# A two-layer graph network on one core: sums carried between spans inside PSUM, one register load per span, transfers addressed in bytes

## The chip, the cores and the metric

The kernel runs on one core of one Trainium2 chip. The metric is the device time of one execution in microseconds. A core has five engines that run side by side, each through its own queue of instructions in order: PE multiplies matrices, DVE and ACT work on rows of data, POOL here issues nothing but gathers (indirect transfers), and SP issues the plain transfers. Engines wait for each other through semaphores. The transfers themselves are moved by 16 DMA engines.

## The reference, cut to what matters

```
h = relu(layernorm(x))
# layer 0
edge_in  = concat(h[src], h[dst], edge_attr)
m        = relu(relu(edge_in @ We1 + be1) @ We2 + be2)
node_msg = relu(relu(concat(h[dst], m) @ Wn1 + bn1) @ Wn2 + bn2)
x1 = x + h + segment_sum(node_msg, dst)
# layer 1
h = relu(layernorm(x1))
H = einsum('ni,rio->rno', h, W)
out = x1 + relu(segment_sum((H[etype, src] + b[etype]) * weight, dst))
```

There are N = 12,500 nodes of 128 floats and E = 400,000 edges, sorted by dst, with 64 edge attributes and 8 edge types. Everything is float32.

## The kernel before

**Tiling.** Edges are taken in chunks of 1024 (8 tiles of 128 edges); three chunks are a span. There are 391 chunks and 131 spans. As edges are sorted by dst, the edges of one span end in at most 128 consecutive nodes, beginning at the span's least dst. So a span sums its messages into a 128-row window `acc` in PSUM with matmuls against one-hot matrices (L467 in layer 0, L937 in layer 1). Neighbouring spans share a node where their edges meet: a window of the next span begins on a row that the span before has already added to. The window's place is known only at run time: the least dst of each chunk (`cidx`, already times 3) and of each span (`span`) lie in SBUF, and SP loads them into registers.

**Preamble (0 to about 130 us).** It builds tables of projected nodes (`tab_a`, `tab_cb`), the ends of the chunks, `cidx`, `span`, and a flag `bad` for inputs on which the fast path does not hold. A slower path (`again`) follows under that flag and is not entered with these inputs.

**Layer 0 (about 130 to 5430 us, L698–L728 and its end to L775).** One iteration i of the loop works on chunks i to i-3 at once. POOL gathers chunk i (L357, 8 gathers of 128 rows into `gb`, buffers for 16 chunks; DVE's L402 transposes them and frees them). PE and ACT run the edge network through `pre` (L395, L397), `h` (L410), `pm` (L417), `em` (L422), `u` (L428, L431), `h` (L434), `pq` (L441); DVE adds and multiplies (L449, L455), builds the one-hot matrices (L381, L460), and PE sums the chunk into `acc` (L467). At the end of a span:

- DVE adds the window's old sums `aw`, loaded from `agg0_d` (L474), and the two halves of `acc` into `a20` (L479, L480); SP stores `a20` back to `agg0_d` (L656). This is how a shared row reaches the next span. For that `agg0_d` is filled with zeros first, by 25 transfers of 256 KB (L690–L693).
- `rows_h` (L508–L530) makes x1 = x0 + a20 (L511) and stores it to `x1_d` (L512), normalises it, multiplies by the 8 weight matrices (L520, L528, L529), and stores 128 rows of 8 x 128 floats to `tab_h` (L530).

SP's queue in one span of layer 0, in its order: tab_h (L530), agg0_d (L656), x1_d (L512), then for the coming chunks eats (edge attributes of a span, 768 KB, L555, 3 buffers), relb (756 KB, L557), win (L377, three), xt (L643) and aw (L474): 10 transfers. Each row number is a register load (L549 for each chunk, L639 for the span), and each transfer with a row number has address arithmetic in registers before it. That makes 37 instructions in one row, which all stand behind tab_h's wait for DVE's ht (L529).

**Layer 1 (about 5430 to 9827 us, `layer1_once`, L903–L988).** POOL gathers 8 tiles of `tab_h` rows (512 bytes each) per chunk (L963, buffers for 5 chunks), DVE weighs and adds them (L970, L974), and PE sums the two end segments into `acc` (L937). Per span SP loads the row number (L952), xw from `x1_d` (L956) and aw from `agg_d` (L944), stores agg_d (L806) and out (L809). DVE adds aw and both halves of acc (L804, twice) and makes out (L808).

**Order.** `in_order` (L92–L101) fixes the order of SP, DVE, ACT and PE as the program is written, layer by layer; POOL's order is its program order as well. All buffers are released by semaphores.

Of the kernel before, what the change touches and what calls it, by code (L numbers as in the profile page):

```python
# [11 lines left out]
I32 = mybir.dt.int32  # L12
AF = mybir.ActivationFunctionType
# [9 lines left out]
R = 8  # L23
N = 12500
# [22 lines left out]
NONE = 16384  # L47

@with_exitstack
def gnn_kernel(  # L50
# [33 lines left out]

    nc = tc.nc
# [25 lines left out]
    x1_d = dram.tile([NP + P, D], F32, name="x1_d")  # L111
    agg_d = dram.tile([NP + P, D], F32, name="agg_d")
    tab_h = dram.tile([NP + P, R * D], F32, name="tab_h")
# [29 lines left out]
    cidx = const.tile([1, NCP], I32, name="cidx")  # L143
# [4 lines left out]
    base = const.tile([P, NSP], F32, name="base")  # L148

# [6 lines left out]
    while g < NJ:  # L156
        n = min(GJ if g else 4, NJ - g)
        groups.append((g, n))
        g += n

# [98 lines left out]
    with tc.tile_pool(name="n1", bufs=2) as pool:  # L259
# [56 lines left out]
        nc.vector.tensor_scalar(cidx, los, 3.0, None, op0=OP.mult)  # L316
        nc.vector.tensor_reduce(slo, los.rearrange("o (s c) -> o s c", c=SC), AX.X, OP.min)
        nc.vector.tensor_reduce(shi, his.rearrange("o (s c) -> o s c", c=SC), AX.X, OP.max)
        nc.vector.tensor_copy(span, slo)
# [12 lines left out]
        vs = pool.tile([1, 5], F32, name="vs", bufs=1)  # L332
# [10 lines left out]
        nc.vector.tensor_reduce(vs[:, 2:3], v3, AX.X, OP.max)  # L343
        nc.vector.tensor_copy(vs[:, 3:4], slo[:, 0:1])
        nc.vector.tensor_scalar(vs[:, 4:5], slo[:, NS - 1:NS], -1.0, float(N - P),
                                op0=OP.mult, op1=OP.add)
        nc.vector.tensor_reduce(vm[:, 0:1], vs, AX.X, OP.max)

# [13 lines left out]
    class Edges:  # L362
# [7 lines left out]
        def load(self, c, row):  # L370
            self.eat = self.pool.tile([P, 512], F32, name="eat", bufs=2)
            nc.sync.dma_start(self.eat, ea[ds(c, 1), :, :].rearrange("o k e -> (o k) e"))
            self.load_win(row)

        def load_win(self, row):
            self.win = self.pool.tile([WR, 96], BF16, name="win", bufs=8)
            nc.sync.dma_start(self.win, tab_cb[ds(row, WR), :])  # L377

        def ends_T(self):
            self.ohT = self.pool.tile([WR, CE], BF16, name="ohT", bufs=4)  # L380
            nc.vector.tensor_tensor(self.ohT, self.relb, self.node.to_broadcast([WR, CE]),  # L381
                                    op=OP.is_equal)
# [10 lines left out]
        def first(self):  # L393
            self.pre = self.psum.tile([64, 512], F32, name="pre")
            nc.tensor.matmul(self.pre, w_ea, self.eat, start=True, stop=False)  # L395
            for h in range(2):
                nc.tensor.matmul(self.pre[32 * h:32 * h + 32, :], self.win[:, 64:96],  # L397
                                 self.half_T(h), start=False, stop=True)
# [64 lines left out]
        def fifth(self, acc, start, stop):  # L463
            for i in range(CT):

# [3 lines left out]
                                 start=(start and i == 0), stop=(stop and i == CT - 1))  # L469

# [37 lines left out]
    def rows_h(pool, psum, row, x0, aw, banks, to_out=False):  # L508

        x1 = pool.tile([P, D], F32, name="x1", bufs=2)  # L510
        nc.vector.tensor_add(x1, x0, aw)  # L511
        nc.sync.dma_start(x1_d[ds(row, P), :], x1)  # L512
        if to_out:
            nc.sync.dma_start(out[ds(row, P), :], x1)
# [8 lines left out]
        ht = pool.tile([P, R * D], F32, name="ht1", bufs=2)  # L523
# [6 lines left out]
        nc.sync.dma_start(tab_h[ds(row, P), :], ht)  # L530


    with tc.tile_pool(name="e0", bufs=2) as pool, \
# [6 lines left out]
        chunks, spans, loaded = {}, {}, {}  # L540
        active = []

# [3 lines left out]

        def load(c):
            e = Edges(pool, psum, iota_p, nid_p)
            row = nc.values_load(cidx[0:1, c:c + 1], engines=[ENG.SP], min_val=0,  # L549
                                 max_val=3 * (N - 1),  # L550
                                 skip_runtime_bounds_check_because="a chunk's least dst is a node")
            s, k = divmod(c, SC)
            if k == 0:
                eat = pool.tile([P, SC, 512], F32, name="eats", bufs=3)
                nc.sync.dma_start(eat, ea[c:c + SC, :, :].rearrange("c k e -> k c e"))  # L555
                relb = pool.tile([WR, SC, CE], BF16, name="relb", bufs=2)
                nc.sync.dma_start(relb, rel_d[c:c + SC, :].rearrange("(o c) e -> o c e", o=1)  # L557
                                  .to_broadcast([WR, SC, CE]))
                loaded[s] = eat, relb
            eat, relb = loaded[s]  # L560
            e.eat, e.relb = eat[:, k, :], relb[:, k, :]
            e.load_win(nc.s_assert_within(
                row, 0, 3 * (NP - WB), skip_runtime_bounds_check_because="WB < NP - N"))
            chunks[c] = e

        def prepare():
# [5 lines left out]
            for g in range(0, NTP, QT):  # L572
                m = min(QT, NTP - g)
                cols = slice(g, g + m)
                for given, table in ((dst_t, dst_d), (et, hidx_d), (ew, ew_d)):
# [6 lines left out]
                    elif given is et:  # L582
                        nc.vector.scalar_tensor_tensor(raw[:, :m], src_sb[:, cols], float(R),
# [48 lines left out]
            nc.sync.dma_start(x1_d[NP:NP + P, :], zeros[:, 0, :])  # L632
            yield from zero(zeros, agg_d)

        class Span:


            def __init__(self, s):
                self.row = nc.values_load(  # L639
                    span[0:1, s:s + 1], engines=[ENG.SP], min_val=0, max_val=N - 1,  # L640
                    skip_runtime_bounds_check_because="a span's least dst is a node")
                self.xt = pool.tile([P, D], F32, name="xt")
                nc.sync.dma_start(self.xt, x[ds(self.row, P), :])  # L643
# [4 lines left out]
            def begin(self):  # L648
                self.x0 = plus_normed(pool, self.xt, self.mv, self.sd)
                self.aw = window0(pool, self.row, P)  # L650

            def end(self, left):

                a2 = add0(pool, self.aw, self.acc, P)
                if left:
                    nc.sync.dma_start(agg0_d[ds(self.row, P), :], a2)  # L656
                banks = ("u", "u", "u") if left else ("pre", "pm0", "pm1")
                steps = rows_h(pool, psum, self.row, self.x0, a2, banks)
# [7 lines left out]
        def sum_up(c):  # L666
# [5 lines left out]
            chunks.pop(c).fifth(of.acc, k == 0, stop)  # L672
# [15 lines left out]
        for c in range(min(AHEAD, NC)):  # L688
            load(c)
        zeros = pool.tile([P, 4, D], F32, name="zeros", bufs=1)  # L690
        nc.vector.memset(zeros, 0.0)
        for _ in zero(zeros, agg0_d):
            pass  # L693
        chunks[0].ends_T()
# [3 lines left out]
        for i in range(L):  # L698
            if i + AHEAD < NC:
                load(i + AHEAD)  # L700
            if i % SC == 0 and i:
                spans[i // SC - 1] = Span(i // SC - 1)
            gb = gathered(i)
            chunks[i].first()
# [9 lines left out]
            chunks[i + 1].ends_T()  # L714
# [23 lines left out]
        for s in range((L - 1) // SC, NS):  # L738
            if s not in spans:
                spans[s] = Span(s)  # L740
                spans[s].deviate()
        spans[(L - 1) // SC].begin()
        gb = gathered(L)
        chunks[L].first()
# [34 lines left out]
    tab_hr = tab_h[0:N, :].rearrange("n (r o) -> (n r) o", r=R)  # L779
# [13 lines left out]
    def window1(pool, row):  # L793

        aw = pool.tile([P, D], F32, name="aw")
        nc.sync.dma_start(aw, agg_d[ds(row, P), :])
        xw = pool.tile([P, D], F32, name="xw1")
        nc.sync.dma_start(xw, x1_d[ds(row, P), :])
        return aw, xw

    def add_out(pool, aw, xw, accs, row):
        a2 = pool.tile([P, D], F32, name="a2")
        for acc in accs:
            nc.vector.tensor_add(a2, aw, acc)  # L804
            aw = a2
        nc.sync.dma_start(agg_d[ds(row, P), :], a2)  # L806
        o = pool.tile([P, D], F32, name="o")
        nc.vector.scalar_tensor_tensor(o, a2, 0.0, xw, op0=OP.max, op1=OP.add)  # L808
        nc.sync.dma_start(out[ds(row, P), :], o)  # L809
# [22 lines left out]
    def again():  # L832
# [7 lines left out]
        with tc.tile_pool(name="g1", bufs=2) as pool, \  # L840
                tc.tile_pool(name="g1_ps", bufs=1, space=PSUM) as psum:

            def layer0(s):
# [5 lines left out]
                def body(row):  # L849
                    acc = psum.tile([P, 2 * D], F32, name="acc")  # L850
                    for k in range(SC):
                        c = s * SC + k
                        e = Edges(pool, psum, iota_f, nid)
                        e.load(c, row * 3)
                        e.ends_T_of(c, node)
                        e.first()
# [18 lines left out]
            with tc.For_i(0, NP, P) as row:  # L875
# [3 lines left out]
                for _ in rows_h(pool, psum, row, x0, window0(pool, row, P), ("u", "u", "u"),  # L879
                                to_out=True):  # L880
                    pass

        with tc.tile_pool(name="g2", bufs=2) as pool, \
                tc.tile_pool(name="g2_acc", bufs=2, space=PSUM) as accp:

            def layer1(s):
# [4 lines left out]
                def body(row):  # L891
# [4 lines left out]
                    add_out(pool, *window1(pool, row), (acc,), row)  # L896
# [6 lines left out]
    def layer1_once():  # L903


        WS = 4
        with tc.tile_pool(name="e1", bufs=2) as pool, \
# [6 lines left out]
            sums_of = []  # L914
# [16 lines left out]
            def sum_up(acc, sm, hm, rel, begin, stop):  # L931
# [4 lines left out]
                for q in range(2):  # L936
                    nc.tensor.matmul(acc[:, 0:2 * D], oh[:, q, :],  # L937
# [3 lines left out]
            def write():  # L941
                acc, row, xw = sums_of.pop(0)
                aw = pool.tile([P, D], F32, name="aw")
                nc.sync.dma_start(aw, agg_d[ds(row, P), :])  # L944
                return lambda: add_out(pool, aw, xw, (acc[:, 0:D], acc[:, D:2 * D]), row)

            for c in range(NC):
                s, k = divmod(c, SC)
                if k == 0:
                    if s % WS == 0:  # L950
                        w_p = weights(s)
                    row = nc.values_load(  # L952
                        span[0:1, s:s + 1], engines=[ENG.SP], min_val=0, max_val=N - 1,
                        skip_runtime_bounds_check_because="a span's least dst is a node")
                    xw = pool.tile([P, D], F32, name="xw1", bufs=3)
                    nc.sync.dma_start(xw, x1_d[ds(row, P), :])  # L956
                    acc = psum.tile([P, 512], F32, name="acc1", bufs=3)
                    sums_of.append((acc, row, xw))
                    if s:
                        end = write()  # L960
# [18 lines left out]
                todo.append((acc, sm, hm, ends, k == 0, k == SC - 1 or c == NC - 1))  # L979
                if k == SC - 1 and s:  # L980
                    end()
# [76 lines left out]
```

## Time and profile before

| what | us or share |
|---|---|
| median of 3 runs (lowest, highest) | 9830.73 (9818.11, 9840.15) |
| the profiled execution's own time | 9828.86 |
| its span | 9827.1 |
| PE busy; DVE; ACT; POOL | 38%; 54%; 17%; 64% |
| granted PE clock, mean | 0.657 |
| gathers of layer 0 (L357), 3032 of them | 2865.2, 945 ns each |
| gathers of layer 1 (L963), 3128 of them | 3327.2, 1064 ns each |

And the page's busy shares along the span, in 40 slices of 246 us, where a digit is tenths:

```profile
PE   2566666666666666666667100000000000000000
PEld 1223333323333332332333000000000000000000
DVE  4556655555555555555557555555555555555554
ACT  2222222222222222222223000000000000000000
POOL 6555555555555555555552677777777777777776
PEclk6777777777777778777778555555555555555555
DMA  4333333222222222222222222222222222222221
```

The first 22 slices are layer 0, the others layer 1. In layer 0 PE, DVE and POOL are each busy for half to two thirds; in layer 1 POOL leads and PE is nearly idle. A busy share is a mean over a slice: what an engine waits for has to be read from the waits and the timeline. A wait "<-remote" is one whose semaphore event the profile cannot lay to an instruction of this core.

### The profile page before, as it was taken

To read this page: it belongs to the slowest core of one execution; us is meant where nothing else is said; L and a number is where in the kernel's file an instruction comes from. 1 tells how busy PE (TensorE), PEld (TensorE's weight loads), DVE (VectorE), ACT (ScalarE), POOL (GpSimd) and SP (SyncE) were. 2 spreads that over 40 slices of the span, in tenths; PEclk is the share of its full clock that TensorE was granted. 3 is DMA by queue.
4 is the path that set the end of the run, shared out by engine and by line. 5 is a ranking of instruction groups with operands and counts; after the bars stand their busy time and mean duration, and the time that the engine had idled before them with its cause. 6 is when DMAs were issued, how large, how long until landed. Compare 5 with 4: busy or idle time off the path is not lost.

```text
span 9827.1 us, 59273 instructions
## 1 busy us (share of the span) xinstructions
PE 3767.4 (38%) x13461; PEld 1854.1 (19%) x13462; DVE 5327.9 (54%) x8545; ACT 1659.8 (17%) x3217; POOL 6320.1 (64%) x6273
## 2 busy tenths in 40 slices
PE   2566666666666666666667100000000000000000
PEld 1223333323333332332333000000000000000000
DVE  4556655555555555555557555555555555555554
ACT  2222222222222222222223000000000000000000
POOL 6555555555555555555552677777777777777776
PEclk6777777777777778777778555555555555555555
DMA  4333333222222222222222222222222222222221
GB/s 150 75 83 78 76 78 94 75 69 70 69 70 73 75 70 69 70 70 70 69 73 83 59 55 55 55 55 55 55 55 55 55 55 55 55 55 55 55 55 50
DMA packets 706959, 662.00 MB, mean 67 GB/s; under 512 B 372896, under 2 KB 561124, under 8 KB 706142
## 3 DMA queue, kind: packets, MB, share of 16 engines
q1 hardware_dynamic: 504440, 401.06, 13.1%
q0 software_dynamic: 200192, 256.65, 12.3%
q8 instruction: 110, 1.80, 0.1%
q14 instruction: 253, 2.07, 0.1%
q10 hardware_dynamic: 1964, 0.41, 0.0%
HBM read 527.08 MB, written 130.51 MB: 67 GB/s over the span
## 4 chain that ended last, share of the span: by engine, by line
POOL 31%; PE 21%; another core or an unknown queue 18%; issue 18%; DVE 7%; ACT 5%; DMA 1%; SPq 0%; DVEq 0%; ACTq 0%; POOLq 0%
POOL hg L963 31%; PE pq L441 5%; PE pm L417 3%; PE acc L467 3%; PE pre L395 3%; PE u L431 2%; DVE nm L455 2%; ACT em L422 2%; PE u L528 2%; ACT h L434 1%; PE pre L397 1%; ACT h L410 1%; DVE ht L529 1%; PE u L428 1%
## 5 line engine op out<-in xcount | busy, mean ns | idle before, releaser
L357 POOL DMA_INDIRECT gb<-tab_a,src_sb x3032 | 2865.2, 945 | 2220.2 <-DVE agT L402 1359.8
L963 POOL DMA_INDIRECT hg<-tab_h,hidx_sb x3128 | 3327.2, 1064 | 1198.4 <-issue 1001.8
L970 DVE TENSOR_TENSOR v<-hg,io_p 128x1024 f32<-128x1024 f32 x782 | 960.1, 1228 | 2135.4 <-DMA hg<-tab_h,hidx_sb 2127.5
L937 PE MATMUL acc<-hm,oh 128*128 128x256 f32 x782 | 299.8, 484 | 4067.7 <-DVE oh L934 2162.8
L449 DVE TENSOR_TENSOR pq<-pq,b_n 128x512 f32<-128x512 f32 x782 | 529.7, 696 | 1430.2 <-remote 991.7
L937 PEld LDWEIGHTS acc<-hm,oh 128*128 128x128 f32 x782 | 196.0, 311 | 4172.4 <-issue 4138.0
L974 DVE TENSOR_REDUCE sm<-v 128x128 f32<-128x1024 f32 x782 | 959.1, 1227 | 9.0
L441 PE MATMUL pq<-w_n,h 128*128 128x256 f32 x3128 | 871.3, 429 | 0.0
L977 ACT CAST hm<-sm 128x256 fp32r<-128x256 f32 x391 | 145.5, 372 | 4224.2 <-DVE sm L974 3662.8
L455 DVE SCALAR_TENSOR_TENSOR nm<-pq,nm 128x512 fp32r<-128x512 f32 x782 | 503.9, 686 | 600.4 <-ACT nm L450 424.4
L434 ACT ACTIVATE h<-u,b_n 128x512 f32<-128x512 f32 x391 | 268.6, 687 | 2649.9 <-remote 1726.3
L441 PEld LDWEIGHTS pq<-w_n,h 128*128 128x128 f32 x3128 | 663.2, 223 | 95.9 <-issue 0.8
L417 PE MATMUL pm<-h,w_e 32*128 32x512 f32 x1564 | 550.6, 786 | 106.6 <-ACT h L410 71.5
L422 ACT ACTIVATE em<-pm,b_e 128x512 f32<-128x512 f32 x782 | 492.8, 680 | 530.0 <-PE pm L417 399.9
L467 PE MATMUL acc<-nm,oh 128*128 128x256 f32 x3128 | 572.4, 335 | 23.7 <-DVE ht L529 4.9
L395 PE MATMUL pre<-eats,w_ea 128*64 128x512 f32 x782 | 537.5, 776 | 85.8 <-DMA eats<-in_ea 84.8
L467 PEld LDWEIGHTS acc<-nm,oh 128*128 128x128 f32 x3128 | 483.4, 229 | 411.0 <-issue 157.6
L520 PE MATMUL u<-ident,t 128*128 128x128 f32 x130 | 56.8, 437 | 1193.6 <-ACT h L434 1168.0
L528 PE MATMUL u<-w_f,hT 128*128 128x512 f32 x520 | 320.9, 701 | 484.8 <-ACT h L434 359.6
L381 DVE TENSOR_TENSOR ohT<-relb,io_p 126x1024 bf16<-126x1024 bf16 x391 | 477.7, 1222 | 27.3 <-issue 12.0
L460 DVE TENSOR_TENSOR oh<-io_p,rel_s 128x1024 fp32r<-128x1024 f32 x391 | 476.1, 1218 | 0.0
L431 PE MATMUL u<-em,w_msg 128*64 128x512 f32 x1564 | 434.3, 605 | 38.6 <-ACT em L422 19.4
(116 smaller groups left out, 3663.6 us busy)
## 6 DMA issues: line engine op xcount, KB each, us to landing
eats<-in_ea SPq DMA_DIRECT2D x131, 768.0 KB
relb<-rel_d SPq DMA_DIRECT2D x131, 756.0 KB
tab_h<-ht SPq DMA_DIRECT2D x131, 512.0 KB
hg<-tab_h,hidx_sb POOLq DMA_INDIRECT x3128
gb<-tab_a,src_sb POOLq DMA_INDIRECT x3032
aw<-agg_d SPq DMA_DIRECT2D x262, 64.0 KB
agg_d<-a SPq DMA_DIRECT2D x261, 64.0 KB
agg_d<-zeros SPq DMA_DIRECT2D x48, 256.0 KB
```

Of the source, the lines that this page charges most:

```text
L357: nc.gpsimd.indirect_dma_start(out=gb[:, t, :], out_offset=None, in_=tab_a, in_offset=bass.IndirectOffsetOnAxis(ap=idx(t), axis=0))
L395: nc.tensor.matmul(self.pre, w_ea, self.eat, start=True, stop=False)
L417: nc.tensor.matmul(pm, w_e2[rows, :], self.h1[rows, :], start=True, stop=True)
L422: nc.scalar.activation(em, pms[h], AF.Relu, bias=b_e2)
L431: nc.tensor.matmul(u[64 * h:64 * h + 64, :], w_msg, self.em[h], start=False, stop=True)
L441: nc.tensor.matmul(pq[:, 2 * i:2 * i + 2, :], self.h2[:, P * (2 * k + i):P * (2 * k + i) + P], w_n2, start=True, stop=True)
L449: nc.vector.tensor_add(pq, pq, b_n2[:, None, :].to_broadcast([P, 4, D]))
L455: nc.vector.scalar_tensor_tensor(nm[:, :, 1, :], pq, 0.0, nm[:, :, 0, :], op0=OP.max, op1=OP.subtract)
L467: nc.tensor.matmul(acc, self.oh[:, i, :], self.nm[:, at, :, :].rearrange("p q d -> p (q d)"), start=(start and i == 0), stop=(stop and i = ...
L963: nc.gpsimd.indirect_dma_start(out=hg[:, t - c * CT, :], out_offset=None, in_=tab_hr, in_offset=bass.IndirectOffsetOnAxis(ap=hidx_sb[:, t: ...
L970: nc.vector.tensor_tensor(v, hg, w_p[:, q, t:t + CT, None].to_broadcast([P, CT, D]), op=OP.mult)
L974: nc.vector.tensor_reduce(sm[:, q, :], v.rearrange("p t d -> p d t"), AX.X, OP.add)
```

## The change

1. **Carried sums.** The sums of a span stay in SBUF until the next span. A matrix `carried` (128 x spans, made in the preamble) holds in column s a one in the row of the span before which is this span's first row. A matmul `carry`, before the last matmul of the span, adds that row of the old sums to row 0 of `acc`. One DVE reduction (`summed`) adds the two halves of `acc`. `agg0_d` and `agg_d` are no longer read, stored or filled with zeros on the fast path. The flag `bad` gets one more condition: neighbouring spans share at most one node.
2. **x1 in `tab_h`.** A row of `tab_h` has 9 blocks of 128 floats for 8, and the ninth is x1. `rows_h` writes x1 into the ninth block of `ht` and one transfer stores all of it (4608 bytes a row for 4096). Layer 1 reads x1 from there, and gathers by src*9 + type.
3. **One register load per span.** `heads` holds five numbers of each span: the byte offsets of three `win` windows, of the x and of the `tab_h` row. Layer 0 loads the five with one instruction per span, layer 1 two for each of four spans with one instruction per four spans.
4. **Bytes.** Transfers at run-time rows are written as byte ranges, so that the loaded register is the address and no arithmetic is needed.
5. **Loads spread over the loop's steps.** In the program's order the register load and relb of the next span stand at the first chunk of a span, eats of the next span and xt of this one at the second, and a win at each chunk. eats has two buffers for three. In the compiled order of SP, a span of layer 0 reads: tab_h of an earlier span, register load, relb, win, win, eats, xt, win: 7 transfers, one load and some four waits for semaphores.

The core of the diff:

```diff
-    tab_h = dram.tile([NP + P, R * D], F32, name="tab_h")
+    tab_h = dram.tile([NP + P, RX * D], F32, name="tab_h")
...
+    def from_byte(table, first, n, most):
+        row = in_bytes(table)
+        width = row.shape[1]
+        first = nc.s_assert_within(
+            first, 0, most * width, skip_runtime_bounds_check_because="a least dst is a node")
+        return row.rearrange("n d -> (n d)")[ds(first, n * width)].rearrange("(n d) -> n d", n=n)
...
-        nc.vector.tensor_scalar(cidx, los, 3.0, None, op0=OP.mult)
+        nc.vector.tensor_scalar(heads[:, :, 0:SC], los.rearrange("o (s c) -> o s c", c=SC),
+                                3.0 * WIN, None, op0=OP.mult)
...
+        for k, row in enumerate((ROW, RX * ROW)):
+            nc.vector.tensor_scalar(heads[:, :, SC + k], slo, float(row), None, op0=OP.mult)
...
+        nc.vector.tensor_sub(carried[:, 1:NSP], base[:, 1:NSP], base[:, 0:NSP - 1])
+        nc.vector.tensor_scalar(carried[:, 1:NSP], carried[:, 1:NSP], at, None, op0=OP.is_equal)
...
-    def add0(pool, aw, acc, n):
-        a2 = pool.tile([P, D], F32, name="a20", bufs=2)
-        nc.vector.tensor_add(a2[:n, :], aw[:n, :], acc[:n, 0:D])
-        nc.vector.tensor_add(a2[:n, :], a2[:n, :], acc[:n, D:2 * D])
-        return a2
+    def carry(acc, s, sums):
+        nc.tensor.matmul(acc[0:1, 0:D], carried[:, s:s + 1], sums, start=False, stop=False)
+
+    def summed(pool, acc, name):
+        sums = pool.tile([P, D], F32, name=name, bufs=2)
+        nc.vector.tensor_reduce(sums, acc[:, 0:2 * D].rearrange("p (q d) -> p d q", q=2),
+                                AX.X, OP.add)
+        return sums
...
-        x1 = pool.tile([P, D], F32, name="x1", bufs=2)
+        ht = pool.tile([P, RX * D], F32, name="ht1", bufs=2)
+        x1 = ht[:, R * D:]
         nc.vector.tensor_add(x1, x0, aw)
-        nc.sync.dma_start(x1_d[ds(row, P), :], x1)
...
-        nc.sync.dma_start(tab_h[ds(row, P), :], ht)
+        nc.sync.dma_start(to, in_bytes(ht))
...
+        def head(s):
+            if s < NS:
+                _, rows[s] = nc.values_load_multi_w_load_instructions(
+                    heads[0:1, s, :], engines=[ENG.SP], min_val=0, max_val=RX * ROW * (N - 1),
+                    skip_runtime_bounds_check_because="a least dst is a node")
...
         for i in range(L):
-            if i + AHEAD < NC:
-                load(i + AHEAD)
-            if i % SC == 0 and i:
-                spans[i // SC - 1] = Span(i // SC - 1)
+            s, k = divmod(i, SC)
+            if k == 0:
+                head(s + 1)
+                load_relb(s + 1)
+            load(i + AHEAD)
+            if k == 1:
+                load_eat(s + 1)
+                spans[s] = Span(s)
...
-                aw = pool.tile([P, D], F32, name="aw")
-                nc.sync.dma_start(aw, agg_d[ds(row, P), :])
-                return lambda: add_out(pool, aw, xw, (acc[:, 0:D], acc[:, D:2 * D]), row)
+                acc, to, xw = open_s.pop(0)
+                before[0] = summed(pool, acc, "a2")
+                to_out(pool, before[0], xw, to)
```

## The prediction

> **What bounds the kernel now.** I read the windows by stage first, because the page's shares average two layers with different limits, then the waits, then the timeline of one stall.
>
> Busy time by stage (us, instructions in brackets, then PE's granted clock, DMA share, GB/s):
>
> ```profile
> core 0: us, PE busy (x) PEld busy (x) DVE busy (x) ACT busy (x) POOL busy (x), PEclk, DMA share, GB/s
> 187.00:255.00 68.00, 11.74 (x30) 5.34 (x30) 5.53 (x8) 3.63 (x6) 51.50 (x55) 0.53 0.10 14
> ...
> 2600.00:5180.00 2580.00, 1689.99 (x6111) 802.02 (x6111) 1462.91 (x2637) 721.38 (x1353) 1458.99 (x1544) 0.79 0.25 70
> 5280.00:5406.00 126.00, 108.19 (x462) 52.63 (x460) 105.63 (x194) 54.48 (x99) 0.00 (x0) 1.00 0.28 96
> 5800.00:9600.00 3800.00, 259.86 (x678) 169.91 (x678) 1921.27 (x2460) 126.13 (x339) 2907.15 (x2715) 0.50 0.21 55
> ```
>
> 2600–5180 us is layer 0 in its steady state: no engine is busy for more than two thirds. At 5280 POOL has issued its last layer-0 gather; the same work then runs with PE and DVE 85% busy and the clock at 1.00. Spans of three chunks, counted from one ACT h L434 to the next but two, take 39.9 us in the steady state (38.8 to 40.5) and 25.3 us in this last stretch. A gather is 0.94 us and 0.30 us to the next, 1.249 us; 24 of them need 30.0 us per span. So layer 0 is 10 us per span above its slowest engine.
>
> ```profile
> engine line waited for: us in total, times, longest us
> ...
> ACT h L434 <- remote: 1726.3, 129, 59.4
> POOL gb L357 <- DVE agT L402: 1359.8, 244, 17.6
> ...
> DVE pq L449 <- remote: 991.7, 180, 40.9
> ```
>
> "remote" is a wait that no local instruction explains. In one stall, DVE is through with L498 at 3031.8 us and its next line is
>
> ```profile
> 3041.03 1.46 DVE L449 TENSOR_TENSOR pq<-pq,b_n 128x512 f32<-128x512 f32 x2 [9.19 <-remote]
> ```
>
> The matmuls that it waits for (L441, L431) were issued by 3030.8; their semaphore increments come only at 3041.0–3041.9. During this, SP works off its span's burst at some 0.7 us an instruction, 37 of them in 18.0 us:
>
> ```profile
> 3026.91 0.69 SPq L656 DMA_DIRECT2D agg_d<-a  x1
> 3030.46 0.71 SPq L512 DMA_DIRECT2D x_d<-x  x1
> 3033.29 0.69 SPq L555 DMA_DIRECT2D eats<-in_ea  x1
> ```
>
> (with no gathers, at 5300, the same burst takes 8.0 us and its transfers 0.34–0.51 us). POOL gathers without a gap from 3019.2 to 3038.9, and the increments come 2.1 us after its end. So POOL, SP and PE's increments are in each other's way. Who causes it decides this case.
>
> Three places say **POOL alone suffices**. (1) In the window 187–255 POOL gathers without a pause, SP issues nothing from 186.8 to 285.7, DMA share is 0.10, and PE still has only 30 matmuls in 68 us; DVE waits 40.87 us for one increment. (2) At 1762.1 POOL starts 16 gathers while SP is still: its bursts are 1741.8–1761.1 and 1788.5–1802.7. Yet DVE's L449 waits there:
>
> ```profile
> 1779.72 0.70 DVE L449 TENSOR_TENSOR pq<-pq,b_n 128x512 f32<-128x512 f32 x1 [4.47 <-remote]
> 1784.62 0.70 DVE L449 TENSOR_TENSOR pq<-pq,b_n 128x512 f32<-128x512 f32 x1 [4.20 <-remote]
> ```
>
> The wait starts 13.1 us after POOL's start, against 12.6 us where SP's burst lies in the run. (3) Where the burst lies early in the run (SP 543.4–551.1, POOL 544.0–563.7) DVE waits later, 6.7 us from 561.7, but POOL's pause after it is 10.4 us instead of 7.4. The cycle explains itself without SP: PE and DVE consume a chunk in 8.4 us, POOL fills one in 10.0, so POOL's work joins into runs of 16 gathers; some 13 us into such a run increments stop until POOL is out of buffers.
>
> A rule speaks against this reading. The Trainium skill, "SBUF — State Buffer", section "Who interferes with whom", has it that only the SBUF ports which DVE and GpSimd share can make two operations slow each other; PE never waits on another engine. By that rule POOL cannot hold PE, SP's burst would be the suspect, and cutting it would free layer 0 to POOL's 30.0 us: 9.9 x 122 spans = 1208 us. By the row of 187–255, with SP silent and PE starved, it frees nothing. I follow the row.
>
> Layer 1 (5430–9827) is POOL's own: 3128 gathers at 1.40 us against the floor of 1.249; DVE L970 waits for them.
>
> **The change, part by part.**
>
> *Layer 0, SP's queue.* Per span it loses the aw load (L474), the agg store (L656), the x1 store (L512), the address arithmetic and three of four register loads: 37 instructions become 12, seven of them transfers (tab_h, relb, eats, xt, three win). Still one burst, since all queue behind tab_h's wait for DVE's ht. At 0.7 us an instruction it takes 8–9 us instead of 18.0. Nothing waits for SP's loads in the steady state (DVE L487 <- xt 34.0 us in all). The cover that hides SP is thus whole with or without this: gain 0 if POOL alone sets the stall, up to the stall's 9.2 us per span if SP sets it. I take 0, by the 187–255 row.
>
> *The register load.* One load now brings five registers. The skill's "DMA: Bandwidth & Descriptors" (Latency and other measured facts) gives a load a floor of about 600 ns, by which four loads to one save 1.8 us a span; "Runtime: NRT & Kernel Launch" (Instruction fetch mechanics) gives about 200 ns for each register even in bulk, by which five registers are 1.0 us against 0.8 for four: nothing is saved. The trace has only one-register loads, median 0.455 us (L549) and 0.700 (L952), which include both. I let one be 0.5–1.0 us: it is on SP, hidden in either case.
>
> *Carried sums.* DVE loses two adds (L479, L480: 0.278 + 0.287 us) for one reduce of 256 elements a partition. L974 reduces 1024 in 1.227 us, so a quarter is 0.31; with a fixed part 0.31–0.45. DVE gains 0.1–0.25 us. PE gains a 128x1 by 128x128 matmul, nearest L520 at 0.437 us (L467, wider, 0.335). It needs the sums of a span earlier, 30 us old: no wait. Net in layer 0 from -0.25 to +0.44 us a span; as PE's chain sets when the next agT frees POOL's buffers, I take +0.1: +13 us. In layer 1 PE is 7% busy: 0.
>
> *Layer 1, SP.* aw and its reload order go, so do the agg_d store and the arithmetic; two transfers and a load every fourth span are left: some 4.25 instructions for 15. This touches the bound, for POOL's gathers lengthen beside SP's activity:
>
> ```profile
> 7017.28 0.35 SPq L806 DMA_DIRECT2D agg_d<-a  x1
> 7019.44 0.71 SPq L809 DMA_DIRECT2D out<-o  x1
> ```
>
> ```profile
> 7016.54 0.94 POOL L963 DMA_INDIRECT hg<-tab_h,hidx_sb  x1 [0.30 <-issue]
> 7018.23 1.93 POOL L963 DMA_INDIRECT hg<-tab_h,hidx_sb  x1 [0.75 <-issue]
> 7020.47 1.10 POOL L963 DMA_INDIRECT hg<-tab_h,hidx_sb  x1 [0.30 <-issue]
> ```
>
> Split over 5450–9800 us: 1815 gathers within 1.4 us of an SP instruction come every 1.449 us, 363 us in all above 1.249; 1309 others every 1.313, 83 us above. If the excess follows instructions, 72% of 363 goes: 260 us. If it follows transfers, half: 182. If being near SP is chance (PE and DVE work at the same time), 0. I take 180, since what lengthens above lies beside transfers.
>
> *Others.* x1 goes into tab_h's row (4608 bytes for 4096) and layer 1 reads 128 pieces of 512 bytes as before; a gather still takes 512 bytes. No row of before has the new pitch: bounds ±0.05 us a gather, ±156 us; I take 0, the row of L963. Of the zero fill, 25 transfers (SP 132.8–150.5) leave the start. The first span ends only with POOL's first run (269 us): 0 to 20, I take 10. eats has two buffers for three; it is loaded a span (40 us) ahead, while 768 KB at layer 0's 70 GB/s is 11 us: 0. The new checks and tables add about ten DVE operations of 0.2–0.55 us (L317–L345): +3 us.
>
> *Sum*, against the profiled execution: 9828.9 + 13 + 3 - 180 - 10 = 9655, rounded to **9650 us**. The profiled run is 1.9 us below the median of the runs, span 9827.1: no correction.
>
> **The rivals.**
>
> *A, the stall was SP's and goes.* For it: SP's slow stretch sits in every steady-state stall. Against: 187–255 and 1762–1785. Layer 0 runs at POOL's 30.0 us plus 2%, 30.6: 9.3 x 122 = 1135; 9829 - 1135 - 190 + 16 = 8520 us.
>
> *B, the stall shortens.* In the start (300–610 us) bursts of 12 instructions inside a POOL run came with waits of 4.5–5.8 us three times and 9.2 once. At 4.6 us less per span: 561 us off the forecast, 9090 us. Against: spans there took 43 us on average, not less.
>
> *C, slower: the phase is lost.* The best cadence, 8 + 16 gathers per span, is held while span and POOL's runs keep step. In the disturbed stretches spans take 46.7, 41.3, 41.1, 42.6 us, 3.0 above 39.9. If SP's long burst is what holds the step, every span pays: +366 - 174 = 10,020 us. It decides from 174/122 = 1.4 us per span. Against: after each disturbance the old cadence came back within five spans.
>
> *D, nothing.* Layer 1's excess stays, its gathers being slow for another reason: 9830 us.
>
> **How the numbers follow.** My forecast 0.52 (9560–9740, from layer 1's 260 and from half of 180), A 0.12, B 0.15, C 0.14, D 0.07. The range leaves out A and the worse half of C: 9060 to 9930. Faster by over 0.2% (20 us, what these runs, 22 us apart, can tell): 0.52 + 0.12 + 0.15 = 0.79; within: 0.07; slower: 0.14.
>
> **What would show it.** If I am right, the new profile has layer-0 spans of 39–41 us, remote waits at L434's and L449's counterparts as before (1500–1800 and 900–1000 us), SP's burst down to 12 instructions, and layer 1's gather period at 1.34. A layer-0 span of 30–36 us makes me wrong and SP the culprit; 42 or more, C; a layer-1 period still at 1.40, D.

## The result and the profile after

The kernel after takes 9812.76 us (median of 20 runs, 9778.59 to 9843.29), the kernel before 9830.61 us in 20 runs beside it: ratio 0.9977, 95% interval 0.9966 to 0.9988. The change is worth 12 to 33 us of 9831; forecast were 180. The profiled execution took 9814.24 us with a span of 9812.5. From here on "before" and "after" alone stand for the two kernels.

The windows of the kernel after, in the columns of those of before:

```profile
2600.00:5180.00 2580.00, 1719.45 (x6273) 815.18 (x6273) 1460.62 (x2588) 724.51 (x1358) 1465.26 (x1553) 0.79 0.23 68
5280.00:5406.00 126.00, 110.17 (x475) 53.34 (x473) 109.16 (x202) 53.27 (x100) 0.00 (x0) 1.00 0.23 79
5800.00:9600.00 3800.00, 351.77 (x904) 188.08 (x904) 1927.94 (x2349) 126.12 (x339) 2862.33 (x2715) 0.50 0.18 51
```

Both stages are as before. POOL gets through the same 2715 gathers in the same 3800 us of layer 1, and layer 0 is still a stage in which no engine is busy for more than two thirds. The DMA share is lower, and PE has more records, those of `carry`. The kernel's waits (total us, times, longest):

```profile
ACT h L459 <- remote: 1713.0, 133, 48.3
...
POOL gb L387 <- DVE agT L427: 1348.6, 244, 23.0
...
DVE pq L474 <- remote: 1089.3, 220, 40.9
```

In the kernel before they were 1726.3, 1359.8 and 991.7 us. A burst of SP in one of the stalls, and DVE's line after it:

```profile
3032.10 0.36 SPq L567 DMA_DIRECT2D tab_h<-ht  x1
3034.74 0.38 SPq L595 DMA_DIRECT2D relb<-rel_d  x1
3036.00 3.50 SPq L402 DMA_DIRECT2D win<-tab_cb  x2
...
3045.15 0.70 DVE L474 TENSOR_TENSOR pq<-pq,b_n 128x512 f32<-128x512 f32 x1 [7.46 <-remote]
```

SP's 37 instructions have become 17, but they still take 13.7 us (18.0 before), since each waits longer, and the stall is 7.5 us where it was 9.2. The span does not become shorter for it: spans 32 to 111 take 39.81 us on average against 40.10.

Where the 14.6 us between the two spans lie, by the first and last gather of each layer: layer 0's last gather comes 7.6 us earlier (5265.8 for 5273.3), the step from it to layer 1's first gather is 5.8 us shorter (167.3 for 173.1), layer 1's gathers take 4352.2 us for 4352.3, and the tail behind the last one 27.2 for 28.3.

The experiments met the kernel before, with the program unchanged, at two levels from one group of runs to the next, about 9830 to 9857 us as in the result (called the upper level here) and about 7955 us (the lower level), so each experiment is compared only with the kernel before in its own group.

### The profile page after: what moved, and what is told of

The parts are those of the page before. It is cut to its first block, busy times and chain, and to the rows that moved or that the text cites. A ratio compares the mean times of both kernels' runs of the same rounds, so it can differ in the third digit from the quotient of the medians.

```text
span 9812.5 us, 56126 instructions
## 1 busy us (share of the span) xinstructions
PE 3925.3 (40%) x13981; PEld 1895.2 (19%) x13982; DVE 5313.4 (54%) x8291; ACT 1657.7 (17%) x3217; POOL 6275.8 (64%) x6273
## 4 chain that ended last, share of the span: by engine, by line
POOL 32%; PE 20%; another core or an unknown queue 17%; issue 17%; DVE 8%; ACT 4%; DMA 2%; DVEq 0%; POOLq 0%; SPq 0%; ACTq 0%
POOL hg L1019 31%; PE pq L466 5%; PE acc L494 3%; PE pm L442 3%; PE pre L420 3%; DVE nm L480 2%; ACT em L447 2%; PE u L456 1%; ACT h L459 1%; DMA hg<-tab_h,hidx_sb 1%; PE u L565 1%; PE pre L422 1%; ACT h L435 1%; DVE ohT L406 1%
## 5 line engine op out<-in xcount | busy, mean ns | idle before, releaser
L1019 POOL DMA_INDIRECT hg<-tab_h,hidx_sb x3128 | 3282.0, 1049 | 1237.7 <-issue 994.2
L994 PE MATMUL acc<-hm,oh 128*128 128x256 f32 x782 | 347.7, 512 | 3963.6 <-DVE oh L989 3435.6
L494 PE MATMUL acc<-nm,oh 128*128 128x256 f32 x3128 | 615.5, 343 | 4.1 <-DVE nm L480 2.8
```

The source lines that it names most:

```text
L494: nc.tensor.matmul(acc, self.oh[:, i, :], self.nm[:, at, :, :].rearrange("p q d -> p (q d)"), start=(start and i == 0), stop=(stop and i = ...
L994: nc.tensor.matmul(acc[:, 0:2 * D], oh[:, q, :], hm[:, q, :, :].rearrange("p r d -> p (r d)"), start=begin and q == 0, stop=stop and q == 1)
L1019: nc.gpsimd.indirect_dma_start(out=hg[:, t - c * CT, :], out_offset=None, in_=tab_hr, in_offset=bass.IndirectOffsetOnAxis(ap=hidx_sb[:, t: ...
```

## Experiments

**At the lower level.** The first group had before at 7954.5 us. *SP nearly silent in both loops:*

```diff
-            if s < NS:
+            if s:
+                eats[s] = eats[0]
+            else:
                 eats[s] = pool.tile([P, SC, 512], F32, name="eats", bufs=2)
...
-                    open_s.append((acc, from_byte(out, at_x, P, N - 1),
-                                   x1_of(pool, from_byte(tab_h, at_h, P, N - 1))))
+                    if s == 0:
+                        xw0 = x1_of(pool, from_byte(tab_h, at_h, P, N - 1))
+                    open_s.append((acc, in_bytes(out[min(96 * s, N - P):min(96 * s, N - P) + P, :]),
+                                   xw0))
```

> The kernel after with SP nearly silent in both loops: register load, relb, eats, win, xt and xw are loaded once and used for all spans, and tab_h and out are stored at fixed rows; one store and its wait per span is left (layer 0: 2 instructions for 12, 0.6 MB per span for 2.1 MB). It leaves out the loading of most edge attributes, windows and x rows, so its output is not the reference's. Theory POOL (runs of gathers alone hold back PE's increments, SP is a victim; layer 1's pace is the gathers' own): layer-0 spans stay at 39-42 us, remote waits of ACT's h 1500-1800 us, layer 1 at 1.40 us per gather, time within 1.5% of 9813. Theory SP (its burst sets the stall): layer-0 spans 30-33 us, time 8600-9000. If layer 1's excess follows SP's transfers: 1.30 us per gather or less, 300 us less in layer 1.

7949.3 us, ratio 0.9993 (0.9984 to 1.0002): nothing to gain from SP at this level.

*Fewer gather buffers* (`name="gb", bufs=16` becomes `bufs=3`):

> The kernel after with gather buffers of layer 0 for 3 chunks instead of 16, so POOL cannot start with a run of 128 gathers. Theory POOL: the first span falls from 140 us to some 50 us as the increments are not held back for the length of that run, steady spans stay at 39-41 us as POOL's runs there are 16 at most: 80-100 us faster, about 9720. Theory SP: the first span stays at 100-140 us (it is the first loads that it waits for), time unchanged at 9813 or slower, as the gathers have less lead.

7987.9 us, ratio 1.0042 (1.0026 to 1.0059): there is no first stall to remove at this level (the first span takes 20.3 us, and 22.6 in after at this level), and with the shorter lead the kernel takes 33 us more.

*Layer 1 with 128-byte rows* (`tab_hq`, a view of the table in pieces of 32 floats, in place of `tab_hr`):

> The kernel after with layer 1 gathering 128 bytes per row instead of 512 (each tile of 128 rows as before, from another view of the table; DVE spreads the 32 columns over 128, so its work is the same). The output is not the reference's. If layer 1's pace of 1.40 us per gather is set by the rows' bytes: 1.25-1.30 us per gather, 310-470 us less. If it is set by the number of rows, by SP's or by DVE's work: 1.40 as before, time 9813 within 0.5%.

7952.1 us, 1.248 us per gather, the same as with 512 bytes at this level.

*A pause after each gather of layer 0*, the edit of all the pause experiments but for the width:

```diff
             nc.gpsimd.indirect_dma_start(
                 out=gb[:, t, :], out_offset=None, in_=tab_a,
                 in_offset=bass.IndirectOffsetOnAxis(ap=idx(t), axis=0))
+            if True:
+                pause = gpool.tile([P, 64], F32, name="pause", bufs=1)
+                nc.gpsimd.memset(pause, 0.0)
...
-        in_order(start, ENG.SP, ENG.DVE, ENG.Activation, ENG.PE)
+        in_order(start, ENG.SP, ENG.DVE, ENG.Activation, ENG.PE, ENG.Pool)
```

> The kernel after with a memset of 128x64 on POOL after each gather of layer 0, and POOL's order fixed like the others'. Theory POOL: the gap between two gathers lets increments through; if the memset takes 0.1-0.3 us, a gather comes every 1.35-1.55 us (32-37 us per span), and if the stall goes with it, spans fall from 39.9 to 33-37 us, 350-850 us faster. If only the pace and not the gap matters (the stall remains): spans of 41-46 us, slower by 200-700 us. Theory SP: stall stays with SP's burst, spans at 40-43 us.

8064.6 us, ratio 1.0141 (1.0124 to 1.0158): gathers are 1.28 us apart, which is 97 of the 110 us more.

*The two kernels themselves:*

> The kernel after, unchanged, beside the kernel before on one chip again. The first experiments' chip ran the kernel before in 7954.5 us, without remote waits and at 1.248 us per gather in layer 1, while the runs of the result took 9831. If this run meets a chip like the first one (before at about 9830): ratio 0.997-0.999. If it meets one like the last (before at about 7955): POOL bounds both layers with 6256 gathers at 1.249 us, so theory POOL-bound expects the ratio at 0.999-1.000 (only the start can move), and theory SP-cost (each SP instruction lengthens gathers) expects 0.98-0.99.

> The kernel before, for its trace on this chip. On a chip with before at about 7955: gather period 1.249 us in both layers, layer-0 spans 30.4 us on average, SP's burst of 37 instructions in 8-11 us and no remote waits of several us. On a chip with before at about 9830: as in the profile of before.

After 7957.8, before 7958.8 us: ratio 1.000 (0.9991 to 1.0008). Here the kernel before has no remote waits at all, its SP burst of 37 instructions takes 8.0 us, and layer 1 of the kernel before goes on like this from its first gather to its last, with starts 1.24 to 1.32 us apart:

```profile
6000.39 0.94 POOL L963 DMA_INDIRECT hg<-tab_h,hidx_sb  x1 [0.30 <-issue]
6001.64 0.94 POOL L963 DMA_INDIRECT hg<-tab_h,hidx_sb  x1 [0.30 <-issue]
```

POOL's 6256 gathers at 1.249 us are 7814 of the 7955 us. At this level POOL bounds both layers and SP cannot matter. Repeats of the silent SP (7957.3 beside 7958.8, 7948.2 beside 7955.9 us) and of the 128-byte rows (7950.4) said the same. *The pause with 256 columns:*

> The kernel after with a memset of 128x256 on POOL after each gather of layer 0 (64 columns took 168 ns and made the period 1.28 us). Where before takes about 9830 us: if the gap between gathers lets increments through, spans of 34-37 us and 350-700 us faster than after; if the stall stays, 41-46 us per span. Where before takes about 7955 us: POOL is the bound, a period of 1.42-1.47 us expected, so 3128 x 0.2 = 550-700 us slower than 7955.

8563.7 us: 1.44 us per gather, 608 us slower.

**At the upper level.** *SP nearly silent*, before at 9829.2 us:

> The kernel with SP nearly silent in both loops, in search of a chip on which before takes about 9830 us (it leaves out most loads, the output is not the reference's). There: theory POOL expects layer-0 spans at 39-42 us, 1.40 us per gather in layer 1 and 9700-9850 us; theory SP expects 8600-9000. Where before takes about 7955: 7950, no news.

9742.2 us in one run, and its trace answers the main question. Windows of that kernel, then DVE between two of SP's bursts, which are 2 instructions long and lie at 2901.7–2904.6 and 2941.9–2944.8:

```profile
2600.00:5000.00 2400.00, 1606.72 (x5892) 760.50 (x5888) 1368.69 (x2426) 680.52 (x1273) 1375.06 (x1454) 0.80 0.11 25
5800.00:9500.00 3700.00, 342.37 (x880) 183.10 (x880) 1876.76 (x2283) 123.32 (x331) 2786.06 (x2644) 0.50 0.19 49
```

```profile
2926.65 1.30 DVE L474 TENSOR_TENSOR pq<-pq,b_n 128x512 f32<-128x512 f32 x2 [9.49 <-remote]
```

With SP silent and the DMA share of layer 0 at 0.11 for 0.23, DVE still waits 9.49 us for PE's increments. POOL gathers from 2903.8 to 2923.8, and the increments come 2.9 us after the end of that run. Spans 32 to 111 take 39.65 us. Rival A is refuted. Layer 1 has 2644 gathers in 3700 us, 1.399 us each, with SP silent too. Spans 2 to 31 are 39.8 us for 41.3 in the kernel after; that is 44 of the 70 us that silence is worth against after's 9812.

*3 buffers and 128-byte rows in one kernel*, before at 9856.6 us:

> The kernel after with two edits in separate layers: layer-0 gather buffers for 3 chunks instead of 16, and layer 1 gathering 128 bytes per row instead of 512 (output not the reference's). Where before takes about 9830 us: the first span falls from 140 us to 40-60 us, if POOL's first run of 128 gathers is what holds it; layer 1 falls from 1.40 to 1.25-1.30 us per gather if the rows' bytes set its pace, and stays at 1.40 if the number of rows or something outside the gather does. Where before takes about 7955 us: 7985, as with 3 buffers alone.

9786.6 us. The first span falls from 140.5 to 38.7 us: POOL's first run of 128 gathers made that stall. Of these 102 us only 32 are left at the end of layer 0 (ACT's last h at 5382.3 for 5414.5). Spans 2 to 31 take 14 us more (41.8 us each for 41.3), and the last six take 73 us more: in the kernel after POOL is 16 chunks ahead and done, and five of them take 25.2 to 25.5 us each without gathers beside them, while with 3 buffers POOL gathers almost to the end (to 5329.7 for 5265.8) and the five take some 40 us each. Layer 1 keeps its pace, although its DMA traffic falls to 16 GB/s: 1.393 us on average from first to last gather, 33.6 us for 24 in the steady part. The rows' bytes do not set it.

*Pauses in both layers*, same group:

> The kernel after with a memset on POOL after each gather: 128x256 in layer 0, 128x64 in layer 1. Where before takes about 9830 us: layer 1 stays at 1.40 us per gather if that is a cap over time (the memset's 0.03 us fits into it), and rises to 1.43 if the memset adds to it; layer 0's spans fall to 35-37 us if longer gaps let PE's increments through (gathers 1.44 us apart, 34.5 us per span), or rise to 43-47 us if they don't. Where before takes about 7955 us: 8660.

9662.1 us. Layer 0's last gather comes at 4683.6 us for 5265.8. In layer 1 the memsets were not spread but stood in bunches of 13 to 15 (3 us) behind every 8 gathers; what followed from the bunches is of use all the same: within each eight the gathers are 1.25 us apart, with none of the long ones, at 39.3 us for 24. What a memset after each single gather of layer 1 would do was not seen.

*Pause in layer 0 alone*, 256 and 128 columns, before at 9849.2 us:

> The kernel after with a memset of 128x256 on POOL after each gather of layer 0 alone (gathers 1.44 us apart), layer 1 as in after. Theory CAP: where before takes about 9830-9860 us, something lets only one gather per 1.40 us through over time; issued every 1.25 us they starve PE's increments (layer 0) or are held themselves (layer 1), and at 1.44 us nothing is starved. So layer-0 spans of 34.8 us as in the run with both pauses, layer 1 at 1.40 us per gather: about 9662 - 130 x (39.3 - 33.6) = 8920 us, 9% faster than before. Rival: the faster layer 0 there came with the other edits; then no faster than 9600. Where before takes about 7955 us: 8560, slower by 7.6%.

> As the last with a memset of 128x128: gathers 1.33 us apart (64 columns gave 1.28, 256 gave 1.44), 32.0 us per span. Theory CAP: 1.33 is still under the cap of 1.40 us, so where before takes about 9830 us the stalls of several us stay, if rarer: spans of 36-41 us. Rival theory GAP (any gap longer than 0.3 us lets increments through): spans of 32-33 us, 8600 us. Where before takes about 7955 us: POOL-bound, 7955 + 3128 x 0.085 = 8220.

9031.8 us (ratio 0.9178, 0.9126 to 0.9231) and 9553.8 us (0.9709, 0.9654 to 0.9764). In the timeline of the 256-column kernel a gather comes every 1.44 us, and its remote waits are almost gone:

```profile
3001.83 0.34 POOL L392 MEMSET pause<- 128x256 f32 x1
3002.50 0.95 POOL L387 DMA_INDIRECT gb<-tab_a,src_sb  x1 [0.34 <-issue]
3003.45 0.33 POOL L392 MEMSET pause<- 128x256 f32 x1
3003.95 0.95 POOL L387 DMA_INDIRECT gb<-tab_a,src_sb  x1 [0.17 <-issue]
```

```profile
ACT h L462 <- remote: 153.2, 30, 8.0
DVE pq L477 <- remote: 3.4, 3, 2.2
```

Spans 32 to 111 take 34.78 us, POOL's own 24 x 1.445. With 128 columns (1.338 us) the remote waits of h are 1522.2 us and spans take 37.81. A slightly longer gap helps in part only (37.81 for after's 39.81 us). The pace at which the waits go lies between 1.338 and 1.445 us; no run here narrows that. One reservation: in the run with pauses in both layers, with the same edit and the same 1.445 us in layer 0 but in another group of runs, remote waits of h still summed to 1390.8 us (longest 9.7) and spans took 35.56 us.

*The same pause of 216 columns in both kernels*:

> The kernel before with a memset of 128x216 on POOL after each gather of layer 0 (by the three measured widths, gathers 1.41 us apart, just above the cap), so SP's 37 instructions a span stand beside a layer 0 without POOL's stalls. Theory CAP: where before takes about 9830-9860 us, spans of 34.0-35 us, no long remote waits, about 8930-9030. If SP's transfers count against the cap as well, some stalls come back: spans of 35-38 us, 9100-9400. Where before takes about 7955 us: 8450-8480.

> The kernel after with the same pause of 128x216. Theory CAP: spans of 34 us, 24 x 0.03 x 130 = 94 us less than with the pause of 256 columns: about 8930, where before takes about 9830-9860 us. Against the kernel before with the same pause: the same within 0.5% if SP is off the path, 2-4% faster if SP's transfers count against the cap. If 1.41 us is still too short, spans of 36-38 us and 9200-9500. Where before takes about 7955 us: 8440-8480.

These met the lower level: 8462.9 and 8460.0 us beside 7954.2, and before's once more 8462.0. SP's work is hidden there too. Whether it costs anything at the upper level once the stalls are gone was not seen.

## Why the prediction was right or wrong

**What bounds layer 0: right that it is not SP, and shown.** The forecast took 0 for the shorter SP burst, on the window 187–255 in which POOL gathers alone. Spans are 39.81 for 40.10 us in the steady part, and 39.65 with SP silent. But "POOL alone suffices" holds at the upper level only. The same window of the kernel before at the lower level, with as many gathers:

```profile
187.00:255.00 68.00, 53.00 (x207) 26.65 (x206) 51.71 (x91) 24.01 (x44) 51.24 (x56) 0.93 0.49 114
```

PE has 207 matmuls beside them where it had 30. Gathers without a pause are one condition of the stall; the other one, which makes the level, is not known. By the rule of the Trainium skill weighed there ("SBUF — State Buffer", section "Who interferes with whom"), POOL's gathers could not hold PE; the lower level agrees with that (207 matmuls) and the upper does not (30). The 1208 us were the forecast's own step: a rule by which PE waits on no engine does not make SP the suspect either. Of the forecast's three places the third was misread. In POOL's run of 544.0–563.7 DVE's L449 waits from 554.9 already and ACT's L434 from 550.9, both for "remote", so the waits do not come later where SP's burst lies early; that place says nothing for or against SP.

**Layer 1, the term that failed: "If it follows transfers, half: 182 ... I take 180".** It measured 0.1 us. The step that failed is the one from "the gathers beside SP are longer" to "without SP they get shorter": the excess of the gathers follows neither SP's instructions nor its transfers. Split by nearness as in the forecast, after has 226 us of excess beside SP and 220 away from it; before had 363 and 83. Both sums are 446: the excess was moved, not lowered. It can be seen in after's layer 1, while SP is still from 7009.4 to 7038.5:

```profile
7018.58 1.39 POOL L1019 DMA_INDIRECT hg<-tab_h,hidx_sb  x1 [0.30 <-issue]
...
7028.54 1.24 POOL L1019 DMA_INDIRECT hg<-tab_h,hidx_sb  x1 [0.86 <-issue]
7030.08 1.10 POOL L1019 DMA_INDIRECT hg<-tab_h,hidx_sb  x1 [0.30 <-issue]
```

What holds is a sum over time. Over 24 gathers of the steady part the starts are 33.60 us apart on average in before, in after and with SP silent (from 32.9 to 34.3 for single stretches), whatever the order of short and long ones. The rows of the windows have the same number, 2715 gathers in 3800 us or 1.400 us each, before and after. So the trace of before showed the pace, and a sum over fixed numbers of gathers would have shown that it is even, where the forecast sorted single gathers by what lay beside them and took nearness for cause. Rival D, at a chance of 0.07, was right for layer 1: the gathers are slow for another reason. It did not say which.

**The small terms.** The reduction of 256 elements took 0.419 us, within the 0.31–0.45 that were set. The carry shows as two records of 0.337 us each where one of 0.437 was taken. The sum of +13 us for both cannot be told from the spread of the early spans. The register load of five numbers took 2.19 us (median), not 0.5–1.0, and layer 1's of eight took 1.73; four single loads at 0.455 are 1.8. Joining the loads saved nothing in layer 0; SP hid it, as assumed. Of the two rules weighed there the price for each register comes nearer than the floor: 0.22 us a number for eight, and twice that for five. SP's burst came out at 17 instructions and 13.7 us, not 12 and 8–9: semaphore waits were counted too low, and each instruction waits longer. The start: ACT's first h came 12.8 us later (159.2 for 146.5), where +3 and -10 were set; by layer 0's last gather the kernel after is 7.6 us ahead. The new pitch of 4608 bytes left the gathers' sum over 24 at 33.60.

**The stall's cause in layer 0.** Shown at the upper level: it needs no SP, it ends with POOL's runs, it takes 140 us at the start because of a run of 128 gathers, and it all but goes when gathers are 1.445 us apart, though not at 1.338 and not in every run at 1.445. With layer 1 held at 1.400 over time this fits one account: at the upper level something takes one gather of 128 rows in 1.40 us, and POOL issues one in 1.25. In layer 1 POOL itself is held back for the difference; in layer 0 PE's increments and SP are. SP's instructions point the same way. In before, 1182 of its 4455 in layer 0 (500 to 5250 us) and 1037 of its 1695 in layer 1 (5800 to 9600 us) take 0.68 to 0.72 us, which is half of 1.40; with the pause of 256 columns in layer 0 it is 19 of 1464 (1500 to 4500 us), and at the lower level 12 of 3077 (1500 to 3900 us). That it is one thing in both layers is argued, not shown, and the reservation above stands against a sharp threshold. What the thing is stays open; it is not the rows' bytes (128 and 512 give 33.6) and not SP. Nor are the transfers themselves slower: the gathers' packets take 12.3% of 16 engines' 9827 us in before at the upper level and 14.9% of 7951.5 us at the lower one, 1209 and 1185 us. DVE's share was not tried. Open too is what puts a run on the upper or the lower level. It is not the chip alone: the kernel before took 7954.5 us on chip 4 and half an hour later 9829.2, and on chip 6 9849.2 and then 7954.2.

**A version faster than both.** At the upper level the kernel after with the pause of 256 columns in layer 0 is 8.2% faster than before. At the lower level the same kernel is 7.6% slower (8563.7 beside 7955.9), since there POOL is the bound. It is a remedy for one level only.

## What to carry to other kernels

When single items of a stream are uneven, add them up over a fixed number before looking for what stands beside the long ones: a constant sum points to a cap, and taking neighbours away then moves the excess without making it smaller. Where an engine's increments come late only while another engine issues gathers back to back, slow that issue down before thinning other queues, and see first that the waits are there: where they were not, the same pause cost 7.6%. And a queue that is slow during a stall may be a victim of it: silence it once, and see whether the stall stays.

## What was not expected of the hardware

One program ran at 7955 and at 9830–9857 us in different groups of runs, with runs of one group within 0.7%. At the upper level the core's granted clock is lower as well (0.657 for 0.71) and PE is busy for 38% of the span where it is 44% at the lower. At the lower level a gather of 128 rows costs POOL 1.249 us for 128 and for 512 bytes a row; at the upper level layer 1 pays 1.400 for both. At the upper level, issuing gathers more slowly made a kernel 8% faster.
